# Time attention with one block of scores a step: scores of two groups in one block, the root on ScalarE, VectorE in forms with one SBUF input

## The chip, the cores and the metric

The kernel runs on one core of a Trainium2 chip. The metric is the device time of one execution in microseconds (us), as the median over several runs. The kernel before takes 2787.39 us (3 runs, 2783.62 to 2787.84). "The span" is the length of one profiled execution, 1 to 2 us below the time of the same run.

## The reference, cut to what matters

One block of a network on `x[2, 256, 128, 128]` (batch, time, bands, channels): causal attention over time, attention over bands within 16 neighbours, a feed-forward part. Each has a layer norm ahead and a residual sum behind.

```python
B, T, FB, C = (2, 256, 128, 128)
H_T, H_F, BAND = (4, 4, 16)
xt = _ln(x, ln_t_w, ln_t_b).transpose(0, 2, 1, 3)
x = x + _mha(xt, t_wi, t_bi, t_wo, t_bo, H_T, cm).transpose(0, 2, 1, 3)   # cm: causal over 256 times
xf = _ln(x, ln_f_w, ln_f_b)
x = x + _mha(xf, f_wi, f_bi, f_wo, f_bo, H_F, bm)                          # bm: |i - j| <= 16 over 128 bands
xn = _ln(x, ln_n_w, ln_n_b)
x = x + (jax.nn.gelu(xn @ w1.T + b1, approximate=False) @ w2.T + b2)
```

## The kernel before

Everything works on groups of 512 columns. There are 128 groups of the time attention, then 16 runs of eight groups of the band attention followed by eight of the feed-forward part. A loop over steps issues pieces of several groups in each step, so that the engines work side by side. A time group holds two sequences of 256 times. Per sequence and head the causal scores need 256 columns for the first 128 keys and 128 for the second.

A head has 32 channels. The score products use 32 rows of the array per head, so the four heads stand in four row tiles (the profile writes 32\*128); all other products of the attention use four column tiles (128\*32).

```python
class OverTime(Attention):
    def scores(self, s):                       # one sequence: 256 + 128 columns per head
        ...
        for h in range(H):
            r = rows_of(h)
            path.tensor.matmul(
                self.sp[h][:, 0 : 2 * P], self.kT[r, a : a + P], self.qT[r, a : a + 2 * P], start=True, stop=True
            )
        for h in range(H):
            r = rows_of(h)
            path.tensor.matmul(
                self.sp[h][:, 2 * P : W], self.kT[r, a + P : a + 2 * P], self.qT[r, a + P : a + 2 * P],
                start=True, stop=True,
            )

    def add(self, engine, s):                  # sum of two blocks of weights, for the row sums
        engine.tensor_tensor(self.block(s, 3), self.block(s, 1), self.block(s, 2), ALU.add)
...
    def root(self):                            # 1 / sqrt(var + eps), on GpSimd
        gpsimd.tensor_scalar(self.rstd, self.mv[:, :, 1], EPS, None, ALU.add)
        gpsimd.tensor_tensor(self.rstd, self.rstd, path.k.mhalf, ALU.pow)

    def normalize(self):                       # xh, on VectorE: four rows of 128 elements
        for i in range(NT):
            vector.tensor_scalar(
                self.xh[:, i, :], self.src()[:, i, :], self.mv[:, i, 0:1], self.rstd[:, i : i + 1],
                ALU.subtract, ALU.mult,
            )

    def turn(self):                            # transposition: z, then by DMA to DRAM ("turned") and back ("xnT")
        ...
```

In the band attention, VectorE multiplies the mask of some heads into the weights after the exponential (`second_mask`).

Of the kernel before, what the change touches and what calls it, by code (L numbers as in the profile page):

```python
# [10 lines left out]
F32 = mybir.dt.float32  # L11
# [424 lines left out]
class Group:  # L436
# [32 lines left out]

    def normalize(self):  # L470
        path, vector = self.path, self.path.vector
        self.xh = path.work.tile([P, NT, P], F32, name="xh", bufs=2)
        for i in range(NT):
            vector.tensor_scalar(
                self.xh[:, i, :], self.src()[:, i, :], self.mv[:, i, 0:1], self.rstd[:, i : i + 1],
                ALU.subtract, ALU.mult,
            )

    def turn(self):


        path = self.path
        z = path.work.tile([P, H, P], F32, name="z", bufs=2)
        path.vector.transpose(
            z.rearrange("p c (t q) -> p c t q", q=D), self.xh.rearrange("p t (c q) -> p c t q", q=D)
        )
        self.turned = path.dram.tile([H, D, NT, P], F32, name="turned")
        for i in range(NT):
            path.nc.sync.dma_start(self.turned[:, :, i, :].rearrange("c a x -> a c x"), z[rows_of(i)])
# [21 lines left out]
    def second_mask(self):  # L511
        pass

    def last_sum(self):
        pass
# [32 lines left out]
class Attention(Group):  # L548
    which = None

# [5 lines left out]
    def queries_keys(self):  # L556
        path = self.path
        wf = path.k.wf[self.which]
        self.qp = path.bank([P, NT * P], "qp")
        product(path, self.qp, wf[:, 0:P], self.xnT)  # L560

        self.kp = path.bank([P, NT * P], "kp")
        product(path, self.kp, wf[:, P : 2 * P], self.xnT)
# [11 lines left out]
    def values(self):  # L575
        path = self.path
        wv = path.k.wf[self.which][:, 2 * P : 3 * P]
        self.vp = path.bank([P, NT, P], "vp")
        for i in range(NT):
            product(path, self.vp[:, i], self.xnT[:, i * P : (i + 1) * P], wv)  # L580

    def take_values(self):
        path = self.path
        self.v = path.work.tile([P, NT, P], F32, name="v")
        path.scalar.copy(self.v, self.vp)
# [14 lines left out]
    def divide(self):  # L600
# [8 lines left out]
        t = path.work.tile([P, NT * P], F32, name="t", bufs=2)  # L609
        vector.tensor_tensor(by_rows(t), by_tile(self.rp), by_tile(self.r0), ALU.mult)  # L610
        u = path.work.tile([P, NT * P], F32, name="u", bufs=2)
        vector.tensor_tensor(by_rows(u), by_tile(self.op), by_tile(self.r0), ALU.mult)
        self.oT = path.work.tile([P, NT * P], F32, name="oT", bufs=2)
        vector.scalar_tensor_tensor(self.oT, t, 2.0, u, ALU.subtract, ALU.mult)

    def output(self):
        path = self.path
        self.yp = path.bank([P, NT, P], "yp")
# [22 lines left out]
class OverTime(Attention):  # L641




    which = 0
    W = 3 * P

    def scores(self, s):
        path = self.path  # L650
        W, a = self.W, 2 * s * P
        self.sp = [path.bank([P, W], "sp") for h in range(H)]
        for h in range(H):
            r = rows_of(h)
            path.tensor.matmul(
                self.sp[h][:, 0 : 2 * P], self.kT[r, a : a + P], self.qT[r, a : a + 2 * P], start=True, stop=True
            )
        for h in range(H):
            r = rows_of(h)
            path.tensor.matmul(  # L660
                self.sp[h][:, 2 * P : W], self.kT[r, a + P : a + 2 * P], self.qT[r, a + P : a + 2 * P],
                start=True, stop=True,
            )

    def weights(self, s):
        path = self.path
        for h in range(H):
            path.scalar.activation(self.p[:, s, h, 0 : self.W], self.sp[h], AF.Exp)

    def mask(self, s):  # L670
        path = self.path
        for n in (2, 0):
            blk = self.block(s, n)
            path.gpsimd.affine_select(
                out=blk, in_=blk, compare_op=ALU.is_ge, fill=path.zero, base=0,
                pattern=[[0, H], [1, P]], channel_multiplier=-1,
            )

    def block(self, s, n):
        return self.p[:, s, :, n * P : (n + 1) * P]  # L680

    def add(self, engine, s):
        engine.tensor_tensor(self.block(s, 3), self.block(s, 1), self.block(s, 2), ALU.add)

    def first_half(self):
        self.p = self.path.work.tile([P, 2, H, self.W + P], F32, name="pt", tag="p", bufs=2)
        self.scores(0)

    def first_function(self):
        self.weights(0)  # L690

    def first_mask(self):
        self.mask(0)
        self.add(self.path.gpsimd, 0)

    def second_half(self):
        self.scores(1)

    def second_function(self):
        self.weights(1)  # L700

    def second_mask(self):
        self.mask(1)

    def last_sum(self):
        self.add(self.path.vector, 1)

    def weigh_one(self, op, s):
        path, p, v, W = self.path, self.p, self.v, self.W
        for h in range(H):  # L710
            r = rows_of(h)
            path.tensor.matmul(op[r, s, :], v[:, 2 * s, r], p[:, s, h, 0 : 2 * P], start=True, stop=False)
        for h in range(H):
            r = rows_of(h)
            path.tensor.matmul(
                op[r, s, P : 2 * P], v[:, 2 * s + 1, r], p[:, s, h, 2 * P : W], start=False, stop=True
            )

    def weigh(self):
        path = self.path  # L720
        op = path.bank([P, 2, 2 * P], "op")
        rp = path.bank([P, 2, 2 * P], "rp")
        self.weigh_one(op, 0)
        sums = self.p.rearrange("p s h (n q) -> p s h n q", q=P)[:, :, :, 0:4:3, :]
        for h in range(H):
            path.tensor.matmul(rp[rows_of(h), :, :], path.k.ones[:, 0:D], sums[:, :, h], start=True, stop=True)
        self.weigh_one(op, 1)
        self.op = op.rearrange("p s q -> p (s q)")
        self.rp = rp.rearrange("p s q -> p (s q)")


class OverBands(Attention):
# [14 lines left out]
    def first_function(self):  # L747
        for h in range(H):
            self.path.scalar.activation(self.p[:, h].rearrange("p i q -> p (i q)"), self.sp[h], AF.Exp)
# [11 lines left out]
    def second_mask(self):  # L761
        path = self.path
        for h in range(H - self.by_vector, H):
            blk = self.p[:, h]
            path.vector.tensor_tensor(blk, blk, path.band.unsqueeze(1).to_broadcast([P, NT, P]), ALU.mult)

    def first_half(self):
        self.p = self.path.work.tile([P, H, NT, P], F32, name="pf", tag="p", bufs=2)
        self.scores(range(H))

    def weigh(self):
        path = self.path
        self.rp = path.bank([P, NT * P], "rp")
# [13 lines left out]
class FeedForward(Group):  # L787
# [21 lines left out]
    def first_half(self):  # L809
        self.hp = {}  # L810
        self.hT = self.path.work.tile([P, self.path.k.NI, NT * P], F32, name="hT")
# [41 lines left out]
class BoundedPath:  # L853
    def __init__(self, ctx, tc, k):
# [4 lines left out]
        self.ps = ctx.enter_context(tc.tile_pool(name="ps", bufs=8, space=PSUM))  # L859
# [4 lines left out]
        once = ctx.enter_context(tc.tile_pool(name="once", bufs=1))  # L864

        self.band = once.tile([P, P], F32, name="band")
        tc.nc.gpsimd.memset(self.band, 1.0)
        for s in (1, -1):
            tc.nc.gpsimd.affine_select(
                out=self.band, in_=self.band, compare_op=ALU.is_ge, fill=0.0, base=BAND,  # L870
# [3 lines left out]
    def bank(self, shape, name):  # L874
        return self.ps.tile(shape, F32, name=name, tag="ps")
# [12 lines left out]
    def quad(self, held, name, bufs):  # L888

        held[name] = self.xpool.tile([P, NT, NT, P], F32, name=name, tag=name, bufs=bufs)  # L890

    def groups(self, x, out):
# [3 lines left out]
        for b in range(B):  # L896
            for f0 in range(0, FB, GA):
# [17 lines left out]
                def part(name, g, held=held):  # L915
                    if name == "res" and name not in held:
                        self.quad(held, "res", 2)
                    return held[name][:, :, g]
# [3 lines left out]
        for b in range(B):  # L922
            for r0 in range(0, T, RUN):
                run = []
                for t0 in range(r0, r0 + RUN, GB):
# [20 lines left out]
                    def part(name, g, held=held):  # L946
                        if name == "res" and name not in held:
                            self.quad(held, "res", 2)
                        return held[name][:, g]
# [7 lines left out]
    def run(self, x, out):  # L957
# [17 lines left out]
        for n in range(-11, len(groups) + 2):  # L975
            feeds = [at(n - 2 + i, FeedForward) for i in range(5)]
            bands = [at(n - 2 + i, OverBands) for i in range(5)]
            turn = feeds[2] and bands[1]
            self.by_columns = at(n - 1, Attention)
            do(n + 11, "load")  # L980
            do_at(n + 4, OverTime, "statistics")
# [3 lines left out]
            do(n, "first_half", "first_function", "first_mask")  # L985
            if turn:
                do(n, "second_half", "second_function")
            do_at(n + 2, Attention, "fetch")
            do_at(n + 1, FeedForward, "fetch")
            do_at(n + 2, FeedForward, "normalize", "turn")  # L990
            do_at(n + 3, Attention, "normalize", "turn")
            do_at(n + 4, OverTime, "root")
            if bands[2]:
                do(n, "second_mask")
            do(n - 1, "weigh")
            do(n - 1, "invert_exactly" if turn else "invert")
            if bands[2] or turn:
                do(n - 2, "output", "finish")
            do(n - 1, "divide")
            do_at(n + 5, FeedForward, "statistics")  # L1000
            if not turn:
                do(n, "second_half", "second_function")
            if not bands[2]:
                do(n, "second_mask", "bias")
# [3 lines left out]
                if not turn:  # L1008
                    do_at(n + A, OverBands, "statistics", "root")
            do(n + 1, "queries_keys", "take_query", "take_key")  # L1010
            if not bands[2] and not turn:
                do(n - 2, "output", "finish")
            do(n + 1, "values", "take_values")
            do(n, "last_sum")
# [69 lines left out]
```

## Time and profile before

| | before |
|---|---|
| time, median | 2787.39 us |
| span of the profiled run | 2785.18 us |
| fill, to the first row sums of the time attention | 54.38 us |
| first two steps | 16.51 us |
| 117 steady steps of the time attention | 892.32 us, 7.627 each |
| last eight steps of the time attention | 70.54 us |
| from there to the start of the bands | 6.21 us |
| bands and feed-forward, to the end | 1745.21 us |

The rows below the span come from the starts of the row sums (tile `rp`) on TensorE, from one to the next, and add up to the span.

### The profile page before, as it was taken

The numbers are of one execution on the slowest core, as the hardware profiler recorded it, in microseconds if no ns is written. First come the engines' busy times: TensorE is split into PE (matmuls) and PEld (weight loads), VectorE is DVE, ScalarE is ACT, GpSimd is POOL, SyncE is SP. The second block draws the span as 40 slices with busy tenths as digits, with TensorE's granted clock in tenths as the row PEclk, the third lists the DMA queues.
The fourth block names the chain that finished last, engine by engine and source line by source line (L and its number), as shares of the span: only waits on it lengthen the run. The fifth ranks groups of instructions, "written<-read, shape, count | busy, mean of one in ns | idle before, by whom it ended". The sixth has DMA issues, their size and how long they took to land.

```text
span 2785.2 us, 103938 instructions
## 1 busy us (share of the span) xinstructions
PE 2730.3 (98%) x42534; PEld 1867.5 (67%) x42534; DVE 2221.5 (80%) x6446; ACT 1800.0 (65%) x3328; POOL 2079.3 (75%) x2569
## 2 busy tenths in 40 slices
PE   4999999999999989999999999999999999999998
PEld 3666666666666657776777777777777767767776
DVE  5888888888888898778678687687786786876874
ACT  2888888878888866646556556456466465574563
POOL 3899999999999997667676676676676666766762
PEclk9999999999999999999999999999999999999999
DMA  5555555555555554544544544535545445444333
GB/s 121 135 147 137 137 141 143 146 132 146 139 142 135 146 134 117 129 117 102 140 105 111 132 106 123 130 100 127 127 99 137 104 108 130 113 117 114 91 92 85
DMA packets 471301, 343.70 MB, mean 123 GB/s; under 512 B 43296, under 2 KB 405152, under 8 KB 470816
## 3 DMA queue, kind: packets, MB, share of 16 engines
q1 hardware_dynamic: 469568, 335.92, 47.5%
q8 instruction: 337, 5.52, 0.9%
q14 instruction: 148, 1.21, 0.2%
q10 hardware_dynamic: 1248, 1.05, 0.1%
HBM read 169.03 MB, written 167.77 MB: 121 GB/s over the span
## 4 chain that ended last, share of the span: by engine, by line
PE 93%; DVE 3%; DMA 2%; POOL 1%; issue 0%; SPq 0%; ACT 0%; DVEq 0%; POOLq 0%
PE zp L848 17%; PE hp L848 16%; PE sp L848 12%; PE op L848 10%; PE qp L848 8%; PE rp L848 8%; PE vp L848 8%; PE yp L848 7%; PE kp L848 7%; POOL pt L848 1%; DMA x<-in_x 1%; DVE xh L848 1%; DMA xnT<-turned 1%; DVE oT L848 0%; POOL rstd L848 0%; DVE stats L848 0%
## 5 line engine op out<-in xcount | busy, mean ns | idle before, releaser
L848 ACT ACTIVATE hT<-hp,b 128x512 f32<-128x512 f32 x512 | 348.7, 687 | 546.0 <-PE hp L848 536.1
L848 POOL TENSOR_SCALAR_AFFINE_SELECT pf<-pf 128x512 f32<-128x512 f32 x768 | 541.5, 720 | 173.5 <-ACT pf L848 147.1
L848 PEld LDWEIGHTS zp<-w2T_sb,hT 128*128 128x128 f32 x4096 | 476.4, 192 | 56.1 <-issue 54.0
L848 DVE TENSOR_SCALAR xh<-x,mv,rstd 128x128 f32<-128x128 f32 x1536 | 509.2, 392 | 0.4 <-POOL rstd L848 0.4
L848 PE MATMUL zp<-w2T_sb,hT 128*128 128x128 f32 x4096 | 479.8, 275 | 0.1
L848 PE MATMUL hp<-xnT,w1f 128*128 128x512 f32 x1024 | 469.2, 596 | 3.6 <-DMA xnT<-turned 3.4
L848 POOL TENSOR_TENSOR rstd<-rstd,mhalf 128x4 f32<-128x4 f32 x384 | 441.3, 1149 | 32.0
L848 ACT ACTIVATE pt<-sp 128x384 f32<-128x384 f32 x1024 | 419.5, 497 | 58.8 <-PE sp L848 58.8
L848 PE MATMUL sp<-qT,kT 32*128 32x128 f32 (+1 forms) x8192 | 389.5, 315 | 0.8 <-ACT kT L848 0.8
L848 POOL TENSOR_SCALAR_AFFINE_SELECT pt<-pt 128x512 f32<-128x512 f32 x512 | 322.7, 651 | 79.0 <-ACT pt L848 79.0
L848 PEld LDWEIGHTS sp<-qT,kT 32*128 32x128 f32 x8192 | 310.9, 185 | 79.7 <-issue 31.1
L848 POOL TENSOR_SCALAR rstd<-mv 128x4 f32<-128x4 f32 x384 | 89.2, 232 | 365.5 <-DVE mv L848 365.1
L848 DVE BATCH_NORM_STATS2 stats<-x 128x6 f32<-128x128 f32 x1536 | 329.0, 274 | 7.6 <-DMA x<-in_x 7.6
L848 ACT ACTIVATE pf<-sp 128x512 f32<-128x512 f32 x512 | 264.3, 603 | 58.8 <-PE sp L848 52.4
L848 PEld LDWEIGHTS hp<-xnT,w1f 128*128 128x128 f32 x1024 | 182.2, 190 | 178.9 <-issue 109.6
L848 PE MATMUL qp<-xnT,wf 128*32 128x512 f32 (+1 forms) x1856 | 273.1, 600 | 26.2 <-DVE xh L848 26.2
L848 PEld LDWEIGHTS yp<-wn,oT 128*32 128x32 f32 (+1 forms) x7808 | 240.8, 111 | 84.0 <-issue 63.2
L848 PEld LDWEIGHTS vp<-wf,xnT 128*32 128x32 f32 (+1 forms) x7424 | 241.1, 113 | 70.4 <-issue 60.2
L848 DVE STREAM_TRANSPOSE z<-xh 128x512 f32<-128x512 f32 x384 | 273.2, 711 | 18.9 <-DMA turned<-z 5.8
L848 PE MATMUL yp<-wn,oT 128*32 128x128 f32 (+1 forms) x7808 | 277.9, 273 | 0.3 <-DVE t L848 0.3
L848 DVE TENSOR_TENSOR res<-zp,res 128x512 f32<-128x512 f32 x128 | 87.6, 685 | 234.8 <-PE zp L848 234.7
L848 PE MATMUL vp<-wf,xnT 128*32 128x128 f32 (+1 forms) x7424 | 273.5, 273 | 0.5 <-DVE t L848 0.5
(90 smaller groups left out, 4072.8 us busy)
## 6 DMA issues: line engine op xcount, KB each, us to landing
turned<-z SPq DMA_DIRECT2D x1536, 64.0 KB, 2.2
xnT<-turned SPq DMA_DIRECT2D x384, 256.0 KB, 2.8
x<-in_x SPq DMA_DIRECT2D x128, 256.0 KB, 4.8
x<-res SPq DMA_DIRECT2D x256, 128.0 KB, 3.4
x<-x SPq DMA_DIRECT2D x128, 256.0 KB, 4.1
out<-res SPq DMA_DIRECT2D x256, 128.0 KB, 2.4
w1T_sb<-in_w1T ACTq DMA_DIRECT2D x1, 256.0 KB, 3.9
w2T_sb<-in_w2T ACTq DMA_DIRECT2D x1, 256.0 KB, 4.2
```

Of the source, the lines that this page charges most:

```text
L848: return self.tc.keep_in_program_order(emit(*args, **kwargs))
```

## The change

Its intent: the array changes between row tiles (scores) and column tiles (the rest) twice a step instead of four times, because the scores that a step needs come in one block. The block takes the first 256 columns of the group ahead (`new`) and the 128-column part of the group behind (`old`); the pipeline is one step deeper. Two blocks of banks change roles from step to step. To make room on the other engines, GpSimd gives up the power of the root in the time attention (ScalarE takes it by Ln and Exp, VectorE adds one refinement), VectorE gives up one sum to GpSimd, and xh is written in a form of five rows of 32 with gaps.

The diff, cut to its core:

```diff
+    def root_by_scalar(self):
+        path = self.path
+        ln = path.small.tile([P, NT], F32, name="lnv")
+        path.scalar.activation(ln, self.mv[:, :, 1], AF.Ln, bias=path.eps)
+        self.root0 = path.small.tile([P, NT], F32, name="root0")
+        path.scalar.activation(self.root0, ln, AF.Exp, scale=-0.5)
+
+    def refine(self):
+        path, vector, y = self.path, self.path.vector, self.root0
+        t = path.small.tile([P, NT], F32, name="vy")
+        vector.scalar_tensor_tensor(t, self.mv[:, :, 1], EPS, y, ALU.add, ALU.mult)
+        vector.scalar_tensor_tensor(t, t, -0.5, y, ALU.mult, ALU.mult)
+        self.rstd = path.small.tile([P, NT], F32, name="rstd", bufs=16)
+        vector.scalar_tensor_tensor(self.rstd, t, 1.5, y, ALU.add, ALU.mult)
 ...
     def normalize(self):
         path, vector = self.path, self.path.vector
-        self.xh = path.work.tile([P, NT, P], F32, name="xh", bufs=2)
+        row = D + 1
+        run = 5 * row
+        xh = path.work.tile([P, NT * run], F32, name="xh", bufs=2)
+        self.xh = xh.rearrange("p (t c w) -> p c t w", t=NT, w=row)[:, 0:H, :, 0:D]
         for i in range(NT):
+            a = i == NT - 1
+            to = i * run - a * row
             vector.tensor_scalar(
-                self.xh[:, i, :], self.src()[:, i, :], self.mv[:, i, 0:1], self.rstd[:, i : i + 1],
-                ALU.subtract, ALU.mult,
+                xh[:, to : to + run].rearrange("p (c w) -> p c w", w=row)[:, :, 0:D], self.src(i, a * D),
+                self.mv[:, i, 0:1], self.rstd[:, i : i + 1], ALU.subtract, ALU.mult,
             )
 ...   (divide: three passes in another order, each with one input in PSUM and one in SBUF)
-        vector.tensor_tensor(by_rows(t), by_tile(self.rp), by_tile(self.r0), ALU.mult)
+        vector.tensor_tensor(self.rp, self.rp, self.r0, ALU.mult)
         u = path.work.tile([P, NT * P], F32, name="u", bufs=2)
-        vector.tensor_tensor(by_rows(u), by_tile(self.op), by_tile(self.r0), ALU.mult)
+        vector.scalar_tensor_tensor(u, self.rp, 2.0, self.r0, ALU.subtract, ALU.mult)
         self.oT = path.work.tile([P, NT * P], F32, name="oT", bufs=2)
-        vector.scalar_tensor_tensor(self.oT, t, 2.0, u, ALU.subtract, ALU.mult)
+        vector.tensor_tensor(by_rows(self.oT), by_tile(self.op), by_tile(u), ALU.mult)
 ...
+def time_scores(old, new):
+    if new is not None:
+        new.first_tiles()
+    if old is not None:
+        old.second_tiles()
+    for h, second, s in (
+        (0, 1, 0), (1, 0, 0), (2, 0, 0), (3, 1, 0), (0, 1, 1), (3, 1, 1), (0, 0, 0), (3, 0, 0),
+        (1, 0, 1), (2, 0, 1), (0, 0, 1), (3, 0, 1), (1, 1, 0), (2, 1, 0), (1, 1, 1), (2, 1, 1),
+    ):
+        if second and old is not None:
+            old.second_scores(h, s)
+        if not second and new is not None:
+            new.first_scores(h, s)
 ...   (band attention: the mask added to the scores ahead of the exponential)
     def first_function(self):
+        for h in range(H - self.by_vector, H):
+            sp = self.sp[h].rearrange("p (i q) -> p i q", i=NT)
+            path.vector.tensor_tensor(sp, sp, path.band.unsqueeze(1).to_broadcast([P, NT, P]), ALU.add)
 ...
-            path.vector.tensor_tensor(blk, blk, path.band.unsqueeze(1).to_broadcast([P, NT, P]), ALU.mult)
 ...
     def weigh(self):
         path = self.path
+        path.held = dict(yp=path.turn_of_bank(), qp=path.turn_of_bank())
 ...   (the loop over steps)
+            if old is not None or new is not None:
+                time_scores(old, new)
+                b = self.banks
+                Attention.place = dict(rp=b["b0"], op=b["b3"], yp=b["a1"], qp=b["a2"], kp=b["b1"], vp=b["b2"])
 ...
+            if old is not None:
+                old.second_weights(old.late)
+            if new is not None:
+                new.first_weights(new.early)
+            if old is not None:
+                old.second_weights(old.early)
+                old.mask_second()
+                old.add(0)
 ...
+            do_at(n + 5, OverTime, "root_by_scalar", "refine")
+            if at(n - 1, OverTime):
+                do_at(n + A - 1, OverBands, "root_by_scalar", "refine")
```

## The prediction

> **What bounds the kernel now.** I read the page first, then the windows, the waits and the timeline of TensorE. The page's busy shares and chain name one engine:
>
> ```profile
> PE 2730.3 (98%) x42534; PEld 1867.5 (67%) x42534; DVE 2221.5 (80%) x6446; ACT 1800.0 (65%) x3328; POOL 2079.3 (75%) x2569
> ...
> PE 93%; DVE 3%; DMA 2%; POOL 1%; issue 0%; SPq 0%; ACT 0%; DVEq 0%; POOLq 0%
> ```
>
> Busy shares are averages, so I looked at stretches: the time attention, its last steps, and the band attention with the feed-forward.
>
> ```profile
> core 0: us, PE busy (x) PEld busy (x) DVE busy (x) ACT busy (x) POOL busy (x), PEclk, DMA share, GB/s
> 100.00:900.00 800.00, 800.00 (x15941) 504.30 (x15945) 704.60 (x1890) 644.68 (x1365) 736.78 (x839) 1.00 0.54 140
> 971.00:1033.00 62.00, 54.66 (x1075) 34.01 (x1076) 60.87 (x151) 42.51 (x91) 61.17 (x69) 1.00 0.45 113
> 1100.00:2700.00 1600.00, 1596.76 (x21085) 1140.90 (x21088) 1222.69 (x3742) 929.52 (x1526) 1080.23 (x1407) 1.00 0.46 116
> ```
>
> In the first and third TensorE never pauses; in the second it does, and VectorE and GpSimd are the full ones. The waits of TensorE between 100 and 900 us are an empty list. Since matmul ends are modelled, I read only starts. One whole step of the time attention (there are 128) on TensorE:
>
> ```profile
> 500.47 1.07 PE L848 MATMUL qp<-xnT,wf 128*32 128x512 f32 x8
> 501.35 1.04 PE L848 MATMUL kp<-xnT,wf 128*32 128x512 f32 x8
> 502.21 1.06 PE L848 MATMUL yp<-wn,oT 128*32 128x128 f32 x32
> 503.08 1.06 PE L848 MATMUL vp<-wf,xnT 128*32 128x128 f32 x32
> 504.07 0.94 PE L848 MATMUL sp<-qT,kT 32*128 32x256 f32 x16
> 504.93 0.86 PE L848 MATMUL op<-pt,v 128*32 128x256 f32 x16
> 505.61 1.04 PE L848 MATMUL rp<-pt,ones 128*32 128x512 f32 x8
> 506.47 0.83 PE L848 MATMUL op<-pt,v 128*32 128x256 f32 x16
> 507.23 0.94 PE L848 MATMUL sp<-qT,kT 32*128 32x256 f32 x16
> 508.10 0.64 PE L848 MATMUL qp<-xnT,wf 128*32 128x512 f32 x4
> ```
>
> The first column is the start; start to start a step takes 508.10-500.47 = 7.63 us. From the starts of the row sums I listed the length of all steps: two of fill, some 117 of 7.63 us, and the last eight of 8.2 to 9.7 (70.7 in all; they also prepare the first bands). The scores, sp, come in two blocks a step. A product of 512 columns in each quarter of the array takes 0.858 us (kp). A score block has 256+128 = 384 columns in each quarter, so 384/512 x 0.858 = 0.644 would do; it takes 0.865. And the product in front of it is longer: vp takes 0.987 where yp, the same work, takes 0.873; the op in front of the second block takes 0.763 where its own columns need 0.644. The first product behind a block is 0.025 to 0.03 longer (qp 0.883 against kp 0.858). So **entering and leaving a block of scores costs** 0.114 + 0.221 + 0.027 = 0.36 us, whatever its size: the band attention's block of 512 columns takes 1.103, which is 0.245 over 0.858, with the same 0.987 ahead of it.
>
> **What the Trainium skill says.** "TensorEngine Tiling (Array Packing)", Key Properties: "Mode switching requires drain". Scores are 32-row tiles, all else 32-column tiles, so every block is two switches. The trace agrees: 0.36 us for the pair. "SBUF — State Buffer", Who interferes with whom: VectorE shares a port pair with GpSimd, takes it with two SBUF inputs or in a 2-port mode, and the later one blocks for the whole instruction. The trace agrees in kind: xh, a one-input scalar operation, takes 304 to 816 ns, and GpSimd's bias add is 1.27 us or 1.72. "VectorE: DVE Perf Modes", Mode 2×_2P: source and destination must both be in SBUF with outermost dimensions both even, or equal. That explains the odd form of xh: 160 elements in, five rows of 32 out, so the mode is refused and GpSimd is left alone. "ScalarE: Activation LUTs", What ACT_TABLE_LOAD costs: an activation costs about 186 ns + 0.833 ns a column, 93 more with a pointer operand. Four of 384 columns take 1.64 us here, four of 512 in the bands 2.06, or 0.82 ns a column at the margin: it agrees.
>
> **The change part by part.**
>
> 1. Scores of a step in one block: the 256-column part of one group with the 128-column part of the group before it. The columns stay: 768 a quarter, 1.29 us; row sums and weighting keep theirs. One of two pairs of switches goes: 0.36 us of 7.63, all on the path. This rests on the mixed order filling all four quarters: counting 128 and 256 in the listed order, each quarter gets 768 without a hole. New step 7.27, over 117 steps -42.
>
> 2. ScalarE: exponentials become 4 of 512 and 4 of 256; from 0.515 and a line through the two sizes 0.305, 3.28 us together, as 8 x 0.41 now. Root by Ln and Exp on 4 columns: by the skill's formula 0.28 + 0.19, say 0.4 with overlap (estimate). Now it is busy 644.68/800 x 7.63 = 6.15 us a step; then 6.55 of 7.27.
>
> 3. GpSimd loses the power (1.40 and 0.23 in the time window), gains the second sum (1.29) from VectorE. Masks: two of 1024 instead of four of 512; from 292 ns for 128 elements and 610 for 512, 1.04 each (estimate). Sum: 2.1 + 2.6 + 1.3 to 1.7 = 6.0 to 6.4, against 7.02 busy now.
>
> 4. VectorE loses that sum (1.04), gains three tiny ones of the root's refinement (about 0.15 each, as the aggregation's 146 ns). xh: uncontended 270 ns for 64 cycles' worth, so with 160 elements one a cycle 270 - 67 + 167 = 370, four 1.48 us; contended they take 1.39 to 1.8 now, so nothing. The division keeps three passes of about 0.67. From 6.72 busy to about 6.1. None of 2 to 4 is on the path in the steady steps.
>
> 5. Last eight steps: here GpSimd set the pace with two bias adds, root and masks (8.3 us a step start to start). It will hold 2 x 1.04 + 4 x 1.25 = 7.1 and VectorE about 7.3, so I take 7.5 a step: 60 against 70.7, -10.
>
> 6. Bands and feed-forward: TensorE starts come every 6.44 us and every 7.01 us, and none of their products changes. Only the last band steps of each run of eight take 6.57, VectorE being full there; cheaper passes may give -2 in all over 16 runs.
>
> 7. Against it: the pipeline is one step deeper, so a longer fill, +3; and friction where ScalarE at 90% now hands banks over just in time (all eight banks belong to the score block at once), +4, or 0.03 a step. I chose both by judgement.
>
> Sum: -42 - 10 - 2 + 3 + 4 = -47, or 2787.4 - 47 = 2740 us.
>
> **The rivals.**
>
> (a) ScalarE becomes the bound. All eight banks must be read before the block needs them; the last, vp's, is read by ScalarE after the query, key and the new root. Laying its work behind TensorE's starts with 0.25 us from product to reader, the copy of v ends about 8.1 us after the block's start, and its bank is wanted at 7.27 + 0.96 = 8.2. Little slack, so some lateness is possible; for: 90% in order. Against: the author places it last on purpose. It would make the step 7.4: 2756.
>
> (b) VectorE's refinement has two SBUF inputs and must wait three times for GpSimd, which holds the ports in pieces of 1.0 to 1.3 us. Three waits of 0.6 would fill VectorE's 1.1 us of slack and more: step 7.5 to 7.7, 2770 to 2790. Against: not each hits a running add, and the division has nearly a microsecond before its banks are wanted.
>
> (c) The mixed block doesn't pack: matmuls start in program order and a 256 behind a 128 leaves a hole. Every hole of 128 columns costs 0.21 us; two eat the gain. Against: the first four of a block now start within 21 ns of each other, so quarters do run side by side.
>
> (d) Everything frees up: no friction, last steps at 7.3, bands better by 5 us: 2727.
>
> **Range and chances.** The 2% line is 2731.6. The sum without friction and fill reaches 2733, so a clear win needs (d); (a) and a mild (b) stay within 2%; a slower kernel needs (b) or (c) in full and a lost fill, and even then no more than some per cent. Range 2724 to 2766; faster 0.28, within 2% 0.66, slower 0.06.
>
> **What would show it.** Right: starts of the row sums every 7.25 to 7.30 us in the time attention; one sp block a step of about 1.5 us with 0.98 for vp ahead; no waits of TensorE there; steps of bands and feed-forward at 6.44 and 7.01 as before. Wrong: TensorE waiting at the first sp or at rp (for ScalarE's key or v, or GpSimd's sums); a block of 1.7 us or more; VectorE's refinement standing 0.5 us or more behind GpSimd; any change of the band steps.

## The result, and the profile after

The changed kernel takes 2754.10 us (median of 4 runs, 2752.60 to 2757.78) beside 2786.72 us of the kernel before in the runs recorded with it (4 runs, 2783.62 to 2787.84; three of them are those of the first section). The ratio is 0.9887 with a 95% interval of 0.9870 to 0.9904: within 2%, 33 us shorter by the medians, inside the predicted range. A ratio is computed here as the mean time of one kernel's fast runs over that of the other's of the same rounds, so it is not quite the ratio of the medians.

Where the time went, from the two profiled spans. The profiled run of the change was the slowest of its four (2757.78 us), so the spans differ by less than the medians. The expected column takes the terms of the prediction; its friction of +4 is put with the steady steps.

| us | before | after | difference | expected |
|---|---|---|---|---|
| fill, to the first row sums | 54.38 | 57.58 | +3.2 | +3 |
| first two steps | 16.51 | 15.64 | -0.9 | |
| 117 steady steps | 892.32 | 856.41 | -35.9 | -38 |
| last eight steps | 70.54 | 66.19 | -4.4 | -10 |
| to the start of the bands | 6.21 | 7.33 | +1.1 | |
| bands and feed-forward | 1745.21 | 1752.77 | +7.6 | -2 |
| span | 2785.18 | 2755.92 | -29.3 | -47 |

So the steady part came nearly in full, and two smaller parts did not come. The page of the changed kernel, busy time by engine and the chain that ended last:

```profile
PE 2695.7 (98%) x43522; PEld 1880.6 (68%) x43522; DVE 2288.9 (83%) x6727; ACT 1843.3 (67%) x3600; POOL 1861.0 (68%) x2169
...
PE 82%; DVE 11%; DMA 4%; issue 1%; SPq 1%; POOL 1%; ACT 0%; DVEq 0%
```

VectorE (DVE) was 3% of the chain and is 11% now, the DMA was 2% and is 4%. Those are the two places to look at. The windows of the same three stages (columns as in the prediction: stretch, length, busy time of PE, weight loads, DVE, ACT and POOL, then clock, DMA share, GB/s):

```profile
100.00:900.00 800.00, 800.00 (x17502) 558.20 (x17498) 777.13 (x2184) 703.21 (x1641) 645.64 (x548) 1.00 0.56 146
933.00:995.00 62.00, 57.28 (x1118) 38.61 (x1114) 55.29 (x165) 44.79 (x108) 54.38 (x46) 0.92 0.51 127
1100.00:2700.00 1600.00, 1587.42 (x21361) 1107.60 (x21360) 1247.55 (x3723) 935.37 (x1536) 1015.62 (x1408) 1.00 0.44 114
```

In the third line TensorE is busy for 1587.42 of 1600 us, 1596.76 before: it waits more now. In the first line VectorE has gone from 704.60 to 777.13 of 800 us: a step of 7.32 us holds 777.13/800 x 7.32 = 7.11 us of its work, not the 6.1 of the prediction. TensorE shows 800.00 again, although VectorE now sets the pace by a little. This is the case in which a full PE row misleads; the starts decide.

The clock of the second line, 0.92, has to be explained first. In the profiled run of the change the granted clock was 0.50 from 946.1 to 949.5 us and from 983.6 to 990.4 us, both in the last eight steps, and from 2359.2 to 2362.6 us in the bands. The kernel before has no such stretch until its last 6 us. The longest of them:

```profile
983.60:990.40 6.80, 4.82 (x48) 2.93 (x52) 5.38 (x19) 1.89 (x4) 5.57 (x6) 0.50 0.31 88
```

In it the row sums take 1.71 us from their start to the next product's, in place of 0.888. An estimate of the cost is half of the time that TensorE is busy there (3.40, 4.82 and 3.40 us): 4.1 us in the last eight steps and 1.7 in the bands. Two runs shown below support it without an estimate: in e10 and e11 TensorE waits for the same 1.86 us in the last step but one, e10 then has 3.4 us at half the clock and e11 none, and the last step takes 8.95 and 7.27 us. What sets off such a stretch is not shown; the same wait brought it in one run and not in the other. So some us of the last eight steps depend on the run and not on the order of the work alone.

One step on TensorE:

```profile
504.96 1.07 PE L872 MATMUL rp<-p,ones 128*32 128x256 f32 x16
505.85 1.48 PE L872 MATMUL op<-p,v 128*32 128x256 f32 x32
507.15 1.06 PE L872 MATMUL yp<-wn,oT 128*32 128x128 f32 x32
508.02 1.04 PE L872 MATMUL qp<-xnT,wf 128*32 128x512 f32 x8
508.88 1.04 PE L872 MATMUL kp<-xnT,wf 128*32 128x512 f32 x8
509.74 1.06 PE L872 MATMUL vp<-wf,xnT 128*32 128x128 f32 x32
510.73 1.63 PE L872 MATMUL sp<-qT,kT 32*128 32x128 f32 x32
512.28 1.07 PE L872 MATMUL rp<-p,ones 128*32 128x256 f32 x16
```

From row sums to row sums it is 512.28-504.96 = 7.32 us. There is one block of scores, 512.28-510.73 = 1.55 us here; in the quickest steps it is 1.523. With 1.523 the step adds up, start to start, to 0.888 (rp) + 1.300 (op) + 0.873 + 0.859 + 0.858 + 0.987 + 1.523 = 7.288 us. That is what TensorE alone would need; over 117 steps it is 852.7. The remaining 0.03 us a step lies in the score block, and VectorE is its cause:

```profile
503.57 0.69 DVE L872 TENSOR_TENSOR oT<-op,u 128x512 f32<-128x512 f32 x1
503.94 1.27 POOL L872 TENSOR_TENSOR res<-x,orow 128x512 f32<-128x512 f32 x1
504.18 1.06 DVE L872 SCALAR_TENSOR_TENSOR vy<-mv,root 128x4 f32<-128x4 f32 x1
505.27 0.16 DVE L872 SCALAR_TENSOR_TENSOR vy<-vy,root 128x4 f32<-128x4 f32 x1
505.47 0.17 DVE L872 SCALAR_TENSOR_TENSOR rstd<-vy,root 128x4 f32<-128x4 f32 x1
...
506.62 1.58 DVE L872 TENSOR_SCALAR xh<-x,mv,rstd 128x160 f32<-128x160 f32 x4
```

The first small operation of the refinement works on four elements a partition, like the two after it. They take 0.16 and 0.17 us, it takes 1.06: it begins while GpSimd (POOL) adds the bias, and it ends at 504.18+1.06 = 505.24, when that addition has ended (503.94+1.27 = 505.21). VectorE reads the bank of op (`oT<-op,u`) that a late product of the next score block needs, so its late finish stretches the block. A query of xh over all steps between 100 and 900 us, before and after (columns behind the count: least, median and largest duration in ns):

```profile
L848 DVE TENSOR_SCALAR xh<-x,mv,rstd x420: 304/335/816, 101.8 to 895.8; 128x128 f32<-128x128 f32 x140
```

```profile
L872 DVE TENSOR_SCALAR xh<-x,mv,rstd x436: 400/431/443, 104.1 to 895.8; 128x160 f32<-128x160 f32 x146
```

The odd form makes xh even, 400 to 443 ns, and never lets it wait. Its median is 0.1 us above that of before, but some passes before took up to 816 ns, so the means over these passes are close: 417 ns before, 428 after. The median alone would mislead here.

In the second half the products are the same, yet it is 7.6 us longer. The place is the turn from band attention to feed-forward, which comes 16 times: the first product `hp` there needs the transposed input of its group. Before and after, one turn each, from the transposition `z` to that product:

```profile
1073.44 1.07 DVE L848 TENSOR_SCALAR xh<-x,mv,rstd 128x128 f32<-128x128 f32 x4
1074.55 0.71 DVE L848 STREAM_TRANSPOSE z<-xh 128x512 f32<-128x512 f32 x1
1075.19 0.92 DVE L848 TENSOR_TENSOR pf<-pf,band 128x512 f32<-128x512 f32 x1
...
1078.33 1.17 PE L848 MATMUL sp<-qT,kT 32*128 32x128 f32 x32
...
1082.30 1.13 PE L848 MATMUL hp<-xnT,w1f 128*128 128x512 f32 x2
```

```profile
1035.61 0.70 DVE L872 TENSOR_TENSOR sp<-sp,band 128x512 f32<-128x512 f32 x1 [1.09 <-PE sp L872]
1036.22 1.60 DVE L872 TENSOR_SCALAR xh<-x,mv,rstd 128x160 f32<-128x160 f32 x4
1037.86 0.71 DVE L872 STREAM_TRANSPOSE z<-xh 128x512 f32<-128x512 f32 x1
...
1040.66 1.17 PE L872 MATMUL sp<-qT,kT 32*128 32x128 f32 x32
...
1045.37 1.10 PE L872 MATMUL hp<-xnT,w1f 128*128 128x512 f32 x2 [0.79 <-DMA xnT<-turned]
```

Before, z starts 3.78 us ahead of the last score block, after it 2.80. Two things delay it by 0.97 (the mean of the 16 turns): xh takes 1.60 instead of 1.07, and the mask, which stood behind z, now stands ahead of xh and waits for the scores (1.09 us idle). Before, hp starts 7.75 us after z without a wait; after, it starts 7.51 us after z with a wait of 0.79 for the transfer through DRAM, as its bracket says. The first hp of a turn waits for this transfer in 3 of the 16 turns before, 2.7 us in all, and in 12 of them after, 10.8 us in all. The sum over the 16 turns, from the start of the output products `yp` to that of hp, is 19.4 us before and 28.3 after: +8.9. A second, smaller loss: in the first band step of a new run, kp and vp take 0.94 and 1.09 instead of 0.86 and 0.98, since the kept bank of the query is one that was set aside in the run before. That is 0.18 to 0.19 us in each of 16. On the other side, late band steps of a run take 6.44 instead of 6.57 (about -2 in all, as expected). The +7.6 itself compares one trace with one: in the six kernels with the band order of the change (the change, e1, e2, e6, e9, e10) the band part takes 1749.1 to 1754.9 us, which is 3.9 to 9.7 over the single trace of before.

### The profile page after: what moved, and what is told of

Same layout as the page of the kernel before. It is cut to its first block, busy times and chain, and to the rows that moved or that the text cites. A ratio compares the mean times of both kernels' runs of the same rounds, so it can differ in the third digit from the quotient of the medians.

```text
span 2755.9 us, 105739 instructions
## 1 busy us (share of the span) xinstructions
PE 2695.7 (98%) x43522; PEld 1880.6 (68%) x43522; DVE 2288.9 (83%) x6727; ACT 1843.3 (67%) x3600; POOL 1861.0 (68%) x2169
## 3 DMA queue, kind: packets, MB, share of 16 engines
q10 hardware_dynamic: 1248, 1.05, 0.1%
## 4 chain that ended last, share of the span: by engine, by line
PE 82%; DVE 11%; DMA 4%; issue 1%; SPq 1%; POOL 1%; ACT 0%; DVEq 0%
PE zp L872 17%; PE hp L872 16%; PE sp L872 10%; PE op L872 7%; PE rp L872 7%; PE vp L872 7%; PE qp L872 6%; PE kp L872 6%; PE yp L872 6%; DVE xh L872 2%; DVE vy L872 2%; DMA xnT<-turned 2%; DVE u L872 1%; DVE stats L872 1%; DVE res L872 1%
## 5 line engine op out<-in xcount | busy, mean ns | idle before, releaser
L872 POOL TENSOR_SCALAR_AFFINE_SELECT pf<-pf 128x512 f32<-128x512 f32 x768 | 476.9, 635 | 274.8 <-ACT pf L872 248.6
L872 DVE TENSOR_SCALAR xh<-x,mv,rstd 128x160 f32<-128x160 f32 x1536 | 596.2, 430 | 14.1
L872 ACT ACTIVATE p<-sp 128x512 f32<-128x512 f32 (+1 forms) x1024 | 417.3, 501 | 19.9 <-PE sp L872 7.5
L872 POOL TENSOR_SCALAR_AFFINE_SELECT p<-p 128x1024 f32<-128x1024 f32 x256 | 280.2, 1095 | 199.9 <-ACT p L872 199.8
L872 PE MATMUL sp<-qT,kT 32*128 32x128 f32 (+1 forms) x8192 | 363.0, 310 | 5.4 <-DVE oT L872 3.6
L872 POOL TENSOR_TENSOR p<-p,p 128x512 f32<-128x512 f32 x256 | 328.7, 1284 | 10.7
L872 POOL TENSOR_SCALAR rstd<-mv 128x4 f32<-128x4 f32 x248 | 56.3, 227 | 331.9 <-DVE mv L872 330.8
L872 ACT ACTIVATE qT<-qp,bq 128x512 f32<-128x512 f32 x256 | 176.0, 687 | 146.0 <-PE qp L872 146.0
L872 POOL TENSOR_TENSOR rstd<-rstd,mhalf 128x4 f32<-128x4 f32 x248 | 256.6, 1035 | 20.7
L872 PE MATMUL yp<-wn,oT 128*32 128x128 f32 (+1 forms) x7808 | 270.5, 273 | 0.0
```

The source lines that it names most:

```text
L872: return self.tc.keep_in_program_order(emit(*args, **kwargs))
```

## The experiments

Ten kernels, all of one core, all correct and all timed against the kernel before in the same rounds.

### Is it the pair of switches? e1_split_block and e9_split_even

One block is cut in two again, with everything else of the change kept: the last products go behind the row sums. First after 12 of the 16 products:

```diff
-def time_scores(old, new):
+def time_scores(old, new, part):
 ...
-    ):
+    )[12 * part : 12 + 4 * part]:
 ...
+            do_at(n - 1, OverTime, "row_sums")
+            if old is not None or new is not None:
+                time_scores(old, new, 1)
             do(n - 1, "weigh")
```

> The changed kernel with the last four products of the score block moved behind the row sums, so that scores come in two blocks again; nothing else differs. If the gain of the steady steps is one pair of switches of the array (0.36 us), a step grows from 7.32 to about 7.65 us (TensorE's own stream 7.29 + 0.36), over some 120 steps +39 us: about 2793 us, a little above the kernel before. If the gain came from the relief of GpSimd and VectorE instead, TensorE's products still follow each other as before and the step stays near 7.32: about 2754 us.

Measured: 2844.09 us (5 runs), ratio 1.0209 (1.0195 to 1.0223). The steady step is 8.07 us: +0.78 over 7.288, not the 0.36 of a pair. The starts tell why. The twelve products still take 1.523, as the sixteen did: the first twelve leave two quarters of the array with 768 columns and two with 512, and the block lasts as long as its fullest quarter. The second block then takes 0.643 for 256 columns. So the edit added a pair and 256 unhidden columns: rp +0.113, second block 0.643, op +0.024, together 0.78. The expectation was wrong because the cut was uneven, a fault of the experiment. The even cut, after ten products, gives every quarter 512 and then 256 columns:

```diff
-    ):
+    )[10 * part : 10 + 6 * part]:
```

> The first split was uneven: its twelve products put 768 columns on two quarters and 512 on the others, so the block lost 256 columns (0.43 us) besides the switches, which together is the 0.78 us measured. Here the cut is behind the tenth product, where each quarter has had 512. If a pair of switches costs 0.36 us, the step is 7.29 + 0.36 = 7.65 us, and the time 2754 + 117 x 0.33 = 2793 us (range 2789 to 2798). If the split costs for another reason, such as waits for banks, it stays near 8.07 a step and 2840 us.

Measured: 2821.33 us (4 runs), ratio 1.0128 (1.0113 to 1.0144), the steady step 7.87 us. That lies between the two expectations, more than a pair again, and this time the trace shows a wait. TensorE, and one line of ScalarE, in e9:

```profile
505.69 1.16 PE L876 MATMUL sp<-qT,kT 32*128 32x128 f32 x20
506.97 1.07 PE L876 MATMUL rp<-p,ones 128*32 128x256 f32 x16
507.97 0.73 PE L876 MATMUL sp<-qT,kT 32*128 32x256 f32 x12
508.63 0.64 PE L876 MATMUL op<-p,v 128*32 128x256 f32 x8
```

```profile
506.53 1.64 ACT L876 ACTIVATE p<-sp 128x256 f32<-128x256 f32 x4
```

The first block ends at the latest at 505.69+1.16 = 506.85, the row sums start at 506.97. They take over a bank of scores that the first of four exponentials, 506.53 to about 506.94, still reads; in each of 100 steps looked at, they start 0.05 us after it has ended. With 512 columns in each quarter and the excess of 0.236 that the whole block has over its 768 columns (1.523-1.287), the first block would take 0.858+0.236 = 1.09 (an estimate); it takes 1.28 here and 1.31 in the mean, so the wait is 0.21. What is left is the pair: row sums 1.001 against 0.888, the second block 0.657 against its columns' 0.429, op 1.324 against 1.300, together 0.113+0.228+0.024 = 0.365 us. Wait and pair together are the 0.58 by which the step, 7.868, is over TensorE's own 7.288. **The price of a pair is 0.36 us, as predicted from the trace of before, and removing it is the whole of the gain in the steady steps.**

### What does the refinement cost? e2_refine_later, e10_no_refine

e2 issues the three small operations one step later, behind the statistics:

```diff
             do_at(n + 5, OverTime, "statistics")
+            do_at(n + 4, OverTime, "refine")
+            if at(n - 2, OverTime):
+                do_at(n + A - 2, OverBands, "refine")
 ...
-            do_at(n + 5, OverTime, "root_by_scalar", "refine")
+            do_at(n + 5, OverTime, "root_by_scalar")
```

> The changed kernel with the three small refinement operations of the root issued in the next step, behind the statistics, where GpSimd is idle, in place of behind the division, where its bias add holds the ports. If VectorE sets the steady step (it is busy back to back, 7.32 us, of which the first refinement takes 1.06 in place of some 0.15), the step falls to TensorE's own 7.29 and VectorE gets some 0.9 us of idle time; the last eight time steps, 66.2 us, shorten by 3 to 8 us; in all 2744 to 2750 us. If the wait only uses up slack, the time stays at 2754.

Measured: 2754.97 us (4 runs), ratio 0.9886 (the change: 0.9887). Nothing gained, yet two things moved. The steady step became 7.287, TensorE's own sum, and the steady part 852.5 (-3.9): so VectorE did set the 7.32. (The first small operation still takes 0.51 us in the median there, against 1.05 in the change.) But the last eight steps went from 66.2 to 70.3. There the refinement is done for two groups in a step, and in one of these steps, which takes 12.2 us, most of the small operations met GpSimd at work. Four of its six, in e2:

```profile
941.55 0.96 DVE L872 SCALAR_TENSOR_TENSOR vy<-mv,root 128x4 f32<-128x4 f32 x1
...
942.74 1.15 DVE L872 SCALAR_TENSOR_TENSOR rstd<-vy,root 128x4 f32<-128x4 f32 x1
...
943.99 0.94 DVE L872 SCALAR_TENSOR_TENSOR vy<-vy,root 128x4 f32<-128x4 f32 x1
944.97 1.22 DVE L872 SCALAR_TENSOR_TENSOR rstd<-vy,root 128x4 f32<-128x4 f32 x1
```

They stand for 4.3 us where they need 0.6, and TensorE waits 2.69 us for VectorE in that step. About half of the 4 us is the clock: 13.7 us of these eight steps ran at half the clock, 10.2 in the change (by the same estimate, 6.2 us against 4.1). e10 leaves the refinement out: the root by Ln and Exp goes straight to xh. It is less exact and still correct against the reference.

```diff
-        self.root0 = path.small.tile([P, NT], F32, name="root0")
-        path.scalar.activation(self.root0, ln, AF.Exp, scale=-0.5)
+        self.rstd = path.small.tile([P, NT], F32, name="rstd", bufs=16)
+        path.scalar.activation(self.rstd, ln, AF.Exp, scale=-0.5)
 ...
-            do_at(n + 5, OverTime, "root_by_scalar", "refine")
+            do_at(n + 5, OverTime, "root_by_scalar")
```

> The changed kernel without the refinement of the root (less exact on purpose: ScalarE's Ln and Exp alone). VectorE loses three small operations, 1.35 us a step with their waits for GpSimd, and with it the cause that I give for the excess of the steady step over TensorE's stream and for the long last eight steps. If that is right: steady step 7.29 (-3.8 us over 117), last eight steps down from 66.2 by 4 to 8 us, in all 2742 to 2747 us. If the last steps are long for another reason (loads of the first bands, GpSimd's second bias add), only the 3.8 us come: 2750.

Measured: 2745.04 us (4 runs), ratio 0.9854 (0.9839 to 0.9869), as expected. Steady 852.5 (-3.9) and the last eight 60.3 (-5.9): just the 60 that the prediction gave for them. Part of the 5.9 is the clock: by the estimate above, half clock cost the change 4.1 us there and e10 1.7, so the refinement itself is worth about 3.5. The list of waits agrees: in these steps TensorE waits 4.7 us for VectorE in the change and 1.9 in e10. Together with -1.2 in the bands and -1.3 in the first two steps, these are the 12.4 us by which the spans differ. The window of the steady part:

```profile
100.00:900.00 800.00, 800.00 (x17564) 556.69 (x17561) 648.53 (x1868) 706.78 (x1647) 648.48 (x549) 1.00 0.57 147
```

VectorE falls from 777.13 to 648.53. A step of 7.29 us holds 5.9 us of its work now and 7.1 with the refinement: three operations that need 0.5 together occupy it for 1.2, by the wait.

### Is moving the root off GpSimd worth it? e6_root_gpsimd

```diff
-            do_at(n + 5, OverTime, "root_by_scalar", "refine")
+            do_at(n + 5, OverTime, "root")
-                do_at(n + A - 1, OverBands, "root_by_scalar", "refine")
+                do_at(n + A - 1, OverBands, "root")
```

> The changed kernel with the root on GpSimd again (power) in place of ScalarE and VectorE. GpSimd is busy some 6.0 us of a step and gets 1.3 more, without its waits; VectorE falls to 6.0. If GpSimd's load was no bound in the time attention, the step is TensorE's 7.29 and the time 2745 to 2752; if moving the root off it was needed, GpSimd sets a step of 7.4 to 7.6, and the last eight steps 9 to 10 us each: 2775 to 2800.

Measured: 2758.18 us (4 runs), ratio 0.9899 (the change 0.9887), between the two expectations. GpSimd is then nearly full in the steady part, and still nothing waits for it:

```profile
100.00:900.00 800.00, 800.00 (x17576) 556.83 (x17572) 649.39 (x1868) 674.94 (x1429) 781.75 (x769) 1.00 0.57 147
```

781.75 of 800 us, and the step is 7.288. The last eight, where GpSimd also has the bands' work, are 70.0. So the root's move to ScalarE, with its refinement, costs 4 us in the steady steps and saves about as much (70.0 against 66.2) in the last eight; without the refinement it saves 8 to 10 there and costs nothing. Both 70.0 and 66.2 hold half clock, 3.2 and 4.1 us by estimate, so the comparison stands.

### What does the odd form of xh do? e3_xh_two_port

xh is written in four rows of 32 out of 128 elements, into the same layout with gaps:

```diff
-                xh[:, to : to + run].rearrange("p (c w) -> p c w", w=row)[:, :, 0:D], self.src(i, a * D),
+                xh[:, to : to + run].rearrange("p (c w) -> p c w", w=row)[:, a : a + H, 0:D],
+                self.src(i, a * D)[:, a * D : a * D + P],
```

> The changed kernel with xh in four rows of 32 (128 elements) in place of five (160), so that it can take the faster form. If the slower xh (four take 1.6 us, before 1.08) is what makes VectorE late in the band steps, so that the transposed tile reaches TensorE late at each turn to the feed-forward, the band part shortens from 1752.8 to about 1745 us and the runs' last band step falls from 6.4 to 10.2 (mean 7.2) back to 6.5. In the time attention VectorE gains 0.5 us a step but may wait for GpSimd: 7.29 to 7.35. In all 2742 to 2752. If the gaps protect GpSimd in a way that matters, the time steps grow: above 2758.

Measured: 2877.96 us (5 runs), ratio 1.0333 (1.0319 to 1.0347). The steady step is 7.82, the second half 1800.0 us. The same query as above:

```profile
L873 DVE TENSOR_SCALAR xh<-x,mv,rstd x408: 311/730/1461, 103.5 to 893.8; 128x128 f32<-128x128 f32 x136
```

A median of 730 ns instead of 431, with a spread up to 1461: with even rows xh waits for GpSimd's masks and sums. So in the new order the odd form is no decoration. By the means it costs next to nothing in the steady steps against the xh of before (428 against 417 ns), and it saves 1.2 us of VectorE's time a step against the even form in this order by the medians, 1.5 by the means (428 against 807 ns).

### The band part: e5_band_mult, e13_both_bands

e5 multiplies the band mask after the exponential and behind the transposition, as before:

```diff
-        for h in range(H - self.by_vector, H):
-            sp = self.sp[h].rearrange("p (i q) -> p i q", i=NT)
-            path.vector.tensor_tensor(sp, sp, path.band.unsqueeze(1).to_broadcast([P, NT, P]), ALU.add)
 ...
+            if bands[2]:
+                do(n, "second_mask")
```

> The changed kernel with the band mask of the fourth head multiplied onto the exponentials behind the transposition again (two SBUF inputs), in place of added to the scores ahead of the normalisation. If it is this addition, for which VectorE must wait at the head of each band step, that makes the transposed tile late at the turns, the waits for it vanish and the band part shortens by 5 to 8 us: 2746 to 2749. If the slower xh is the cause instead, VectorE's load doesn't fall, and the time stays within 3 us of 2754.

Measured: 2753.48 us (4 runs), ratio 0.9885; the time is that of the change within its scatter, as the second expectation had it. In the trace z starts 3.22 us ahead of the last score block instead of 2.80, so the mask was 0.42 of the 0.97; the other 0.55 is left to the longer xh (0.53 by its durations, not isolated by a run). The 16 turns sum to 22.1 us (28.3), the band part to 1747.9 (1752.8). These two sums flatter e5: its profiled run is the fastest of its four, that of the change the slowest of its four, with 1.7 us of half clock in the bands.

e13 adds the second repair, giving up the kept bank where a run of bands begins:

```diff
+            if feeds[1] and feeds[2]:
+                self.held = {}
```

> The change with the two repairs of its second half and the refinement kept as it is: the band mask multiplied in after the exponential, and the kept bank given up before a run of bands begins. If the 7.6 us that the second half lost are the wait at the 16 turns (the mask alone took 4.9 us off the band part in one trace) and the 0.18 us at each of 16 new runs (2.9 us), the band part goes from 1752.8 to about 1745 and the time from 2754 to 2746-2749. If the runs that start earlier only wait longer for the transposed input at their turns, the second repair gives nothing: band part 1747.5-1749, time 2749-2752.

Measured: 2753.8 us (4 runs), ratio 0.9875 (0.9859 to 0.9892), beside 2788.22 of the kernel before in these rounds. kp and vp are back at 0.86 and 0.98, so that repair works where it applies; but the 16 turns sum to 29.0 us in this trace and the band part to 1750.0. It is nearer to the second expectation, though above its ranges (1747.5 to 1749, and 2749 to 2752 us). The turns scatter by several us from kernel to kernel with the same order of work: the four kernels with the mask behind z show 22.1, 29.0, 25.1 and 23.8, the six with the mask ahead of it 25.7 to 28.3. Each repair can be seen at its place, but neither is proved in the time.

### Put together: e11_best and e12_exact_best

e11 is e10 with both repairs of the band part (their edits are shown above).

> Three edits to the changed kernel together: no refinement of the root, the band mask multiplied behind the exponentials again, and the bank kept for the query product given up when a run of bands has ended (left over, it makes the value product of the next run wait for ScalarE's query, 0.18 us at each of 16 places). If the three losses are what I take them for, they add up: -3.8 in the steady steps, -4 to -8 in the last eight, -2 to -5 at the turns, -2.9 for the bank: 2735 to 2742 us. If the turns wait for the transfers alone, whatever VectorE does, 2740 to 2746.

Measured: 2740.90 us (5 runs, 2738.32 to 2744.10), ratio 0.9838 (0.9824 to 0.9851). It lies where the two expectations overlap (2740 to 2742), so it does not tell them apart. It beats both kernels: steady 852.8, last eight 58.6, band part 1747.6. It is the one changed kernel without half clock ahead of its last few us. Its root is the one without refinement.

e12 keeps the refinement, so it is as exact as the change: the time groups' three operations one step later, the band groups' where they were, with both repairs.

```diff
             do_at(n + 5, OverTime, "statistics")
+            do_at(n + 4, OverTime, "refine")
 ...
-            do_at(n + 5, OverTime, "root_by_scalar", "refine")
+            do_at(n + 5, OverTime, "root_by_scalar")
```

> The same two repairs, and the refinement of the time groups one step later, behind the statistics, while that of the band groups stays directly behind their root. If VectorE sets the steady step only by the refinement's wait of about 1 us, the step goes from 7.32 to 7.29 (-4 us) as it did with both refinements late; with the band groups' refinement not late, the last eight steps should stay near 66 instead of 70. Then 4 us below the run with the two repairs alone: 2742-2746. If the last eight suffer again, nothing is left of it: 2746-2750.

Measured: 2747.98 us (4 runs, 2746.03 to 2750.20), ratio 0.9854 (0.9837 to 0.9870), 6 us below e13 of the same rounds (4 by the profiled spans). The median lies in the range of the second expectation, 2 us above that of the first, but the parts went the way of the first: steady 852.9 (-3.3 against e13), last eight 64.7 (65.3). Without the half clock these would be 63.0 and 62.2 by estimate, so the last eight did not suffer by more than about 1 us. It beats both kernels too, and keeps the exactness.

## Why the prediction was right or wrong

The time lay inside the range, and the mechanism named for the main term was right; the sum was 14 us too low by the medians (2754 against 2740), 18 by the spans (-29.3 against -47). That the time still fell inside the range is in part luck: the bands, for which no loss was allowed, came out 9.6 us above the -2, and the range reaches 26 us above the sum. Point by point:

- **Scores in one block (step 1): right.** 0.36 us a step and 42 in all were expected. By starts, TensorE's own step is 7.288 (7.27 expected), 0.34 below the 7.627 of before, and e9 measured the pair by itself as 0.365. The block packs: 1.523 for 768 columns. Rival (c), holes, is false for this order; e1 shows what holes would have cost (0.43 for 256 columns).
- **ScalarE (step 2): right.** It is busy 703.21/800 x 7.32 = 6.4 us a step (6.55 expected). No TensorE wait stands in the list of waits between 100 and 900 us; rival (a) did not occur.
- **GpSimd (step 3): right.** 645.64/800 x 7.32 = 5.9 us a step (6.0 to 6.4 expected).
- **VectorE (step 4): wrong, and this is the term that was mis-sized.** The prediction gave "about 6.1"; it is 7.1. It charged the three small operations with "about 0.15 each"; the first takes 1.06 because it stands behind GpSimd's addition, as rival (b) and the section cited for it said it might. Leaving the refinement out brings VectorE to 5.9 (e10), so it is the whole of the difference. (The prediction's cost of xh takes one element a cycle of 1.04 ns. The traces agree: 0.16 us for four elements and 0.69 for 512 in the same operation, `vy` and `u`, or about 1.04 ns an element; four xh were put at 1.48 us and take 1.58.) For xh the prediction expected "nothing", and by the means (417 and 428 ns) that held in the steady steps, though not at the turns of the bands, where the four took 1.07 and take 1.60. VectorE's work still just fits, so in the steady steps this costs only 0.03 us, within the friction allowed for, but by another engine than ScalarE, which the prediction had named for it (e2: -3.9 us when it is moved).
- **Last eight steps (step 5): wrong in size**, -4.4 instead of -10, for two reasons. Two groups' refinements meet GpSimd there, which is worth about 3.5 us. And about 4.1 us are half clock, for which the prediction had no term. Without refinement e10 measures 60.3, and e11, which has no half clock either, 58.6; the prediction had said 60. Whether the longer waits for VectorE bring the half clock is not shown.
- **Bands and feed-forward (step 6): wrong**, +7.6 instead of -2. The step that failed goes from "none of their products changes" to a time that stays, and from the reading "in the first and third TensorE never pauses": 3.24 of the 1600 us of the third stretch were pauses, nearly all of them waits of hp for its transfer. The small gain that it expected came. But the change moved the mask ahead of xh and made xh longer, so z came 0.97 us later, and the transfer at the turns, hidden in 13 of 16 before, was waited for in 12 of 16 after. The diff showed both edits. The prediction looked only at the steady pace of these steps and not at the place where a transfer is on the path. How much of the +7.6 is each part isn't settled: the turns account for 8.9 and the kept bank for 3 in this trace, against gains of 2 and scatter, with 1.7 of half clock on top; e5 ties 0.42 of the 0.97 us to the mask.
- **Fill and friction (step 7):** the fill was +3.2 for +3, the friction 0.03 a step as allowed.

The list of what would make it wrong held the two signs that appeared, "VectorE's refinement standing 0.5 us or more behind GpSimd" and "any change of the band steps". Their price was taken as a rival, not as part of the sum.

## What to carry to other kernels

Price a change of the array's tiling from a trace by the starts around it, and remove the change rather than the columns: here the pair was worth 0.36 us of 7.63, with no work saved. An operation of four elements is not cheap by its size: where it reads two tensors from SBUF, charge it with the running GpSimd operation, or put it where GpSimd is idle. When a change reorders work that isn't on the path, follow each transfer that starts behind it to the product that needs it; a delay of 1 us was free in the other band steps and cost the most at the 16 turns. Before a difference of some us in one stage is put down to the code, look at the clock of that stage: the mean of the run, 0.997, hid an 0.92 here.

## What the Trainium skill lacked or had wrong

- "TensorEngine Tiling (Array Packing)", Key Properties, says that a change of mode drains the engine, and that tiles operate independently. It gives no size for the first: here a pair of changes costs 0.36 us, 0.11 in the product ahead, 0.22 in the block of scores and 0.03 behind it. To the second the runs add that a block lasts as long as its fullest quarter: twelve products with 768, 768, 512 and 512 columns took 1.523 us, as much as sixteen with 768 in each.
- "SBUF — State Buffer", Who interferes with whom, says who blocks whom, and for a whole instruction. The runs agree for operations with two SBUF inputs, and show what no example there does: the block doesn't shrink with the operation. Four elements a partition took 0.92 to 1.26 us in place of 0.16, and that helped to fill VectorE to 7.11 us of a step of 7.32.
- No page that was read prices a transfer that comes out from behind other work: with 0.97 us of delay at its start, most steps kept their time and the 16 turns took 8.9 us more in one trace.
